# Attention steps in pairs with two products per step, in place of 64 by 64 quarters

## The chip, the cores and the metric

The kernel runs on one core of one Trainium2 chip. The metric is the device time of one execution in microseconds (us), the median of three runs before the change: 3099.51 us (3098.32 to 3102.71). A core has five engines that run their own instruction queues: PE (matrix products; its weight loads are listed as PEld), DVE (vector), ACT (scalar functions), POOL (general) and SP (which here only issues DMA transfers). Each instruction queue is executed in its order; instructions wait for each other through semaphores.

## The reference

The input is a batch of 8 images of 512 channels by 32 x 32 pixels. Two residual layers follow each other; each computes its output from a group-normalised copy of its input and adds it to that input.

- Layer 0: a group norm, a 1x1 convolution with SiLU (`cv1`), then two bottleneck blocks l = 0, 1. A block is a 3x3 convolution with SiLU, an attention over the 1024 pixels with 4 heads of 64 channels, a 1x1 convolution with SiLU and a residual add. All parts are concatenated and go through a last 1x1 convolution (`cv2`).
- Layer 1: a group norm, a depthwise 3x3 convolution with ReLU, a pruning of weak channels, a 1x1 convolution with ReLU and a second pruning.

The attention is what the change touches:

```
logits = jnp.einsum('bhdi,bhdj->bhij', q, k + r) * HD ** (-0.5)
a = jax.nn.softmax(logits, axis=-1)
out = jnp.einsum('bhij,bhdj->bhdi', a, v)
```

## The kernel before

Everything is fp32. One image is processed at a time. Inside a tile the 128 partitions are channels or, for the attention's exponentials, key pixels. Each fp32 product appears in the trace as two passes (two weight loads and two matmul records).

**The loop over images.** For image b: `cv1`; then for l = 0 and l = 1 the 3x3 convolution `conv3`, the projections `qkv`, `attention` and `cv2m`; between the second `qkv` and the second attention the back of layer 1 for the image before (`layer1_back`), and loads of the next image; then `cv2`. After the loop the last image's layer 1 runs alone.

**Background work.** The front of layer 1 of the previous image (49 pieces: four statistics, one group reduction, four applies, and for each of four channel blocks one start, eight taps and one end) and the group norm of the next image (nine pieces) are lists of closures. `pump` takes pieces off a list between PE instructions: six times per half of `conv3` (one piece each), after each of the six tiles of `qkv` (two pieces), and after each of the four tiles of `cv2` (three pieces). The end of a channel block is a ReLU on ACT, a maximum on DVE and a product on POOL. The group reduction needs two tiny PE products (`pm`, `pv`) with DVE work between them and after them.

**Scheduling.** The tile framework orders each engine's instructions by program order and its own priorities and gives tiles to buffers when it builds the program. So the order on each engine and every wait is fixed before the run; a piece from `pump` may stand somewhat earlier or later than it was written, and it holds its place in its engine's queue.

**Attention.** One call has 32 steps (m, ih, jt): m is a pair of heads, ih one half of the query pixels, jt one of eight blocks of 128 key pixels. Eight steps with one (m, ih) are called a group here; four groups make a call, and 16 calls make the kernel. A step has

- a score product into a PSUM tile of two banks (`ps_s`, from the pool `ps_big` with two buffers), L440: four 64 by 64 quarters of the PE array, one per head a and half c of the key block;
- one exponential of 128 x 1024 on ACT into a tile e of the shared `work` pool (8 buffers), L448;
- one addition of e to the running sum on DVE, L455 (L452 for the first two of a group);
- a value product, L466, for the step two before: again four quarters. The two halves r of the contraction go to two accumulators (`ps_acc`, three buffers).

At a group's end ACT copies one accumulator to SBUF (L476), DVE adds the other to it (L478), and two steps later `finish` multiplies the sums by a matrix of ones (`ps_dn`, L485: two products of 128 rows by 64 columns side by side), copies the denominators by ACT (L490, which also accumulates them for a range check), takes the reciprocal on DVE (L491), passes it once more through ACT for the range check (L492), and scales on DVE (L496).

**Around attention.** `cv2m` (L516) follows at once; its SiLU on ACT needs another function table than the exponential. DVE then adds the residual (L525), which releases the PSUM tile. After l = 0 the transform of `conv3` follows on DVE (L326 to L339); after l = 1 `cv2` (L538) takes the released tile.

Of the kernel before, what the change touches and what calls it, by code (L numbers as in the profile page):

```python
# [8 lines left out]
F32 = mybir.dt.float32  # L9
AF = mybir.ActivationFunctionType  # L10
ALU = mybir.AluOpType
AX = mybir.AxisListType

P = 128
B, C, F = 8, 512, 32
HW = F * F
# [14 lines left out]
def fast_kernel(  # L31
# [21 lines left out]
    dram = ctx.enter_context(tc.tile_pool(name="dram", bufs=1, space=bass.MemoryType.DRAM))  # L53
    small = ctx.enter_context(tc.tile_pool(name="small", bufs=4))
    ps_big = ctx.enter_context(tc.tile_pool(name="ps_big", bufs=2, space=bass.MemoryType.PSUM))
    ps_acc = ctx.enter_context(tc.tile_pool(name="ps_acc", bufs=3, space=bass.MemoryType.PSUM))
    ps_mm = ctx.enter_context(tc.tile_pool(name="ps_mm", bufs=1, space=bass.MemoryType.PSUM))

    def const_tile(shape, name):
        return const.tile(shape, F32, tag=name, name=name)  # L60

    def work_tile(name):
        return workp.tile([P, HW], F32, tag="work", name=name)
# [45 lines left out]
    ones = const_tile([P, HD], "ones")  # L109
    nc.gpsimd.memset(ones, 1.0)  # L110

    rng = const_tile([P, 2 * B * 2 * HEADS], "rng")
    rng_used = [0]
    mhalf = const_tile([P, NBN], "mhalf")
    nc.gpsimd.memset(mhalf, -0.5)
# [267 lines left out]
    def qkv(l, bg, per):  # L383
        for m in range(4):
            ps = ps_big.tile([P, 2, 512], F32, tag="big", name="ps_qk")
            for k in range(2):
                for n in range(2):
                    nc.tensor.matmul(  # L388
                        ps[:, n, :],
                        wqkv_sb[:, k, m * P : (m + 1) * P],  # L390
                        z[:, k, n * 512 : (n + 1) * 512],
                        start=(k == 0),
                        stop=(k == 1),
                    )
            if m < 2:
                nc.scalar.copy(qy[:, m, :], flat(ps))
            else:
                kk = phases(kr[:, m - 2, :])
                full = [P, 4, F, F // 4]
                col = rw[:, l, m - 2, :].rearrange("p (t r) -> p r t", r=4)  # L400
                row = rh[:, l, m - 2, :].unsqueeze(1).unsqueeze(3)
                nc.vector.tensor_tensor(
                    kk, phases(flat(ps)), col.unsqueeze(2).to_broadcast(full), ALU.add
                )
                nc.gpsimd.tensor_tensor(kk, kk, row.to_broadcast(full), ALU.add)
            pump(bg, per)
        for g in range(2):
            ps = ps_big.tile([P, 4, C2], F32, tag="big", name="ps_v")
            for j in range(4):
                jt = 4 * g + j  # L410
                for k in range(2):
                    nc.tensor.matmul(  # L412
                        ps[:, j, :],
                        z[:, k, jt * P : (jt + 1) * P],
                        wqkv_sb[:, k, 2 * C2 : 3 * C2],
                        start=(k == 0),
                        stop=(k == 1),
                    )
            nc.scalar.copy(vt[:, 4 * g : 4 * g + 4, :], ps)
            pump(bg, per)  # L420

    def attention():

        last = HW // P - 1
        steps = [(m, ih, jt) for m in range(2) for ih in range(2) for jt in range(HW // P)]
        es, sm, accs = {}, {}, {}
        quarters = [(r, c) for c in range(2) for r in range(2)]  # L430

        def half(r):
            return slice(r * HD, (r + 1) * HD)

        def scores(s):
            m, ih, jt = steps[s]
            ps = ps_big.tile([P, 2, 512], F32, tag="big", name="ps_s")
            for a, c in quarters:
                j = jt * P + c * HD
                nc.tensor.matmul(  # L440
                    ps[half(c), a, :],
                    kr[half(a), m, j : j + HD],
                    qy[half(a), m, ih * 512 : (ih + 1) * 512],
                    start=True,
                    stop=True,
                )
            e = work_tile("e").rearrange("p (a n) -> p a n", a=2)
            nc.scalar.activation(flat(e), flat(ps), AF.Exp, scale=HD ** -0.5)  # L448
            es[s] = e
            if jt == 1:  # L450
                sm[m, ih] = work_tile("sum").rearrange("p (a n) -> p a n", a=2)
                nc.vector.tensor_tensor(flat(sm[m, ih]), flat(es[s - 1]), flat(e), ALU.add)  # L452
            elif jt:
                t = flat(sm[m, ih])
                nc.vector.tensor_tensor(t, t, flat(e), ALU.add)  # L455

        def values(s):
            m, ih, jt = steps[s]
            if jt == 0:
                accs[m, ih] = [  # L460
                    ps_acc.tile([P, 512], F32, tag="acc", name=f"ps_av{r}") for r in range(2)
                ]
            e = es.pop(s)
            for r, a in quarters:
                h = 2 * m + a
                nc.tensor.matmul(  # L466
                    accs[m, ih][r][half(a), :],
                    vt[half(r), jt, h * HD : (h + 1) * HD],
                    e[half(r), a, :],
                    start=(jt == 0),  # L470
                    stop=(jt == last),
                )
            if jt == last:
                lo, hi = accs.pop((m, ih))
                part = work_tile("part")[:, :512]
                nc.scalar.copy(part, hi)  # L476
                zz = z[:, m, ih * 512 : (ih + 1) * 512]
                nc.vector.tensor_tensor(zz, lo, part, ALU.add)  # L478

        def finish(s):  # L480
            m, ih, _ = steps[s]
            dn = ps_mm.tile([P, 512], F32, tag="mm", name="ps_dn")
            t = sm.pop((m, ih))
            for a in range(2):
                nc.tensor.matmul(dn[half(a), :], ones, t[:, a, :], start=True, stop=True)  # L485

            n = rng_used[0]
            rng_used[0] += 2
            r = work_tile("r")
            nc.scalar.activation(r[:, 512:], dn, AF.Copy, accum_out=rng[:, n : n + 1])  # L490
            nc.vector.reciprocal(r[:, :512], r[:, 512:])  # L491
            nc.scalar.activation(  # L492
                r[:, 512:], r[:, :512], AF.Copy, accum_out=rng[:, n + 1 : n + 2]
            )
            zz = z[:, m, ih * 512 : (ih + 1) * 512]
            nc.vector.tensor_tensor(zz, zz, r[:, :512], ALU.mult)  # L496

        for s in range(len(steps) + 4):
            if s < len(steps):
                scores(s)  # L500
            if 2 <= s < len(steps) + 2:
                values(s - 2)
            if s >= 4 and steps[s - 4][2] == last:
                finish(s - 4)

    def pump(bg, n):

        for _ in range(min(n, len(bg))):
            bg.pop(0)()
# [14 lines left out]
            dst = inner(yp[1], m) if l == 0 else phases(qy[:, m, :])  # L524
            nc.vector.tensor_tensor(dst, phases(flat(ps)), inner(yp[l], m), ALU.add)  # L525

    def cv2(bg, per):
        def rhs(k, n):
            i, m = k // 2, k % 2
            if i in (1, 2):  # L530
                return yp[i - 1][:, 2 * n : 2 * n + 2, m, :, : F // 4]
            return (y0 if i == 0 else qy)[:, m, n * 512 : (n + 1) * 512]

        for m in range(KC):
            ps = ps_big.tile([P, 2, 512], F32, tag="big", name="ps_cv2")
            for k in range(2 * KC):
                for n in range(2):
                    nc.tensor.matmul(  # L538
                        ps[:, n, :],
                        w2_sb[:, k, m * P : (m + 1) * P],  # L540
                        rhs(k, n),
                        start=(k == 0),
                        stop=(k == 2 * KC - 1),
                    )
            act(flat(ps), flat(ps), AF.Silu, BN1 + m)
            nc.vector.tensor_tensor(by_phase(xt[m]), phases(flat(ps)), by_phase(xt[m]), ALU.add)  # L546
            pump(bg, per)

    for w in group_norm(pt, pt):
        w()  # L550
# [1 line left out]
    for b in range(B):  # L552
        cv1()

        bg = layer1_front() if b else []
        conv3(0, bg, 1)
        load_weights(1)
        qkv(0, bg, 2)
        load_qkv(1)
        attention()  # L560
        cv2m(0)
        conv3(1, bg, 1)
        if b + 1 < B:
            load_weights(0)
        qkv(1, bg, 2)
        load_qkv(0)
        pump(bg, len(bg))
        if b:
            layer1_back(b - 1)
        load(xt, b)  # L570
        if b + 1 < B:
            load(pt, b + 1)
            bg = group_norm(pt, pt)
        attention()
        cv2m(1)
        cv2(bg, 3)
        pump(bg, len(bg))
    for w in layer1_front():
        w()
    layer1_back(B - 1)  # L580
# [463 lines left out]
```

## Time and profile before

| What | us |
|---|---|
| median of three runs | 3099.51 |
| time of the profiled execution | 3102.71 |
| span of the profiled execution, first to last instruction | 3100.9 |
| PE busy | 2863.0 (92%) |
| DVE busy | 1858.2 (60%) |
| ACT busy | 988.7 (32%) |
| score products, 4096 records | 557.1 busy, 72.0 idle before them |
| value products, 4096 records | 546.3 busy |

Busy time is the union of an engine's instructions. A row of a timeline merges neighbouring records of one line: its second column is the time from the start of the first to the end of the last of them, and since matmuls overlap, the distance between starts tells how long one takes. The idle time in brackets is followed by what released the engine.

### The profile page before, as it was taken

How to read it: one execution, taken by the hardware profiler on the slowest of the kernel's cores; microseconds unless marked ns; L12 is line 12 of the kernel's file. 1: busy time of each engine (PE TensorE's matmuls, PEld its weight loads, DVE VectorE, ACT ScalarE, POOL GpSimd, SP SyncE). 2: the span in 40 equal slices, each digit the busy share in tenths (PEclk: the TensorE clock that was granted, in tenths of full speed). 3: DMA queues.
4: the chain of work that ended last, by engine and by line, in shares of the span. 5: the costliest groups of instructions: out<-in, count | busy, mean ns of one | idle time of the engine just before them, and what ended most of it. 6: DMA issues, size and time to landing. Idle time of an engine off the chain costs nothing. (4 is left out here: it accounts for less than half of the span.)

```text
span 3100.9 us, 32925 instructions
## 1 busy us (share of the span) xinstructions
PE 2863.0 (92%) x14146; PEld 1448.0 (47%) x14146; DVE 1858.2 (60%) x1995; ACT 988.7 (32%) x1153; POOL 137.0 (4%) x89
## 2 busy tenths in 40 slices
PE   6999999999999999999999999999999999999984
PEld 4453463534645345543555436463363633636331
DVE  6546268572685627756278553775447664576637
ACT  1425124251242413334143331524215241152511
POOL 1000010000100001000010000100001000000000
PEclk9999999999999999999999999999999999999996
DMA  8110010300104001030011200112010120100100
GB/s 348 62 62 11 1 71 1 139 15 0 71 4 149 1 0 72 31 122 1 1 72 62 92 1 31 42 62 92 0 52 21 72 82 1 61 11 24 42 0 28
DMA packets 27513, 155.81 MB, mean 50 GB/s; under 512 B 2784, under 2 KB 7648, under 8 KB 23008
## 3 DMA queue, kind: packets, MB, share of 16 engines
q1 hardware_dynamic: 26352, 149.17, 13.1%
q10 hardware_dynamic: 1008, 4.46, 0.4%
q8 instruction: 113, 1.85, 0.2%
q14 instruction: 40, 0.33, 0.0%
HBM read 127.41 MB, written 26.21 MB: 50 GB/s over the span
## 5 line engine op out<-in xcount | busy, mean ns | idle before, releaser
L440 PE MATMUL ps_s<-qy,kr 64*64 64x512 f32 x4096 | 557.1, 608 | 72.0 <-ACT e L448 36.7
L448 ACT ACTIVATE e<-ps_s 128x1024 f32<-128x1024 f32 x512 | 516.8, 1021 | 246.1 <-PE ps_s L440 246.0
L466 PE MATMUL ps_av<-e,vt 64*64 64x512 f32 x4096 | 546.3, 595 | 0.0
L455 DVE TENSOR_TENSOR sum<-sum,e 128x1024 f32<-128x1024 f32 x384 | 467.0, 1216 | 87.5 <-ACT e L448 75.8
L353 PE MATMUL ps_c<-v,u_sb 128*128 128x248 f32 (+1 forms) x1536 | 350.2, 390 | 42.8 <-issue 39.2
L353 PEld LDWEIGHTS ps_c<-v,u_sb 128*128 128x128 f32 x1536 | 305.2, 199 | 91.1 <-issue 53.3
L440 PEld LDWEIGHTS ps_s<-qy,kr 64*64 64x64 f32 x4096 | 159.7, 135 | 384.2 <-issue 235.2
L250 DVE SCALAR_TENSOR_TENSOR acc<-pt,v_sb,acc 128x961 f32<-128x961 f32 (+1 forms) x256 | 318.9, 1257 | 5.9
L466 PEld LDWEIGHTS ps_av<-e,vt 64*64 64x64 f32 x4096 | 177.8, 134 | 275.0 <-issue 255.7
L546 DVE TENSOR_TENSOR xt<-ps_cv,xt 128x1024 f32<-128x1024 f32 x32 | 64.2, 2005 | 355.5 <-ACT ps_cv L141 355.5
L273 PE MATMUL ps_pw<-pt,wpw_sb 128*128 128x512 f32 x512 | 226.0, 602 | 41.3 <-POOL pt L261 40.6
L491 DVE RECIPROCAL r<-r 128x512 f32<-128x512 f32 x64 | 214.6, 3353 | 26.6 <-ACT r L490 26.6
L388 PE MATMUL ps_qk<-z,wqkv_sb 128*128 128x512 f32 x512 | 224.2, 594 | 5.7 <-ACT z L375 5.7
L292 PE MATMUL ps_cv<-pt,w_sb 128*128 128x512 f32 x512 | 224.1, 599 | 2.3 <-DVE pt L229 2.3
L538 PE MATMUL ps_cv<-yp,w_sb 128*128 128x512 f32 x512 | 224.9, 592 | 0.0
L141 ACT ACTIVATE ps_cv<-ps_cv,bi,sc 128x1024 f32<-128x1024 f32 x32 | 37.7, 1177 | 450.3 <-PE ps_cv L538 450.3
L452 DVE TENSOR_TENSOR sum<-e 128x1024 f32<-128x1024 f32 x64 | 78.4, 1225 | 168.0 <-ACT e L448 168.0
L273 PEld LDWEIGHTS ps_pw<-pt,wpw_sb 128*128 128x128 f32 x512 | 98.8, 194 | 163.7 <-issue 120.3
L353 PE MATMUL ps_c3e<-v,u_sb 128*128 128x248 f32 (+1 forms) x768 | 170.7, 376 | 0.0
L292 PEld LDWEIGHTS ps_cv<-pt,w_sb 128*128 128x128 f32 x512 | 98.3, 192 | 126.3 <-issue 123.4
L538 PEld LDWEIGHTS ps_cv<-yp,w_sb 128*128 128x128 f32 x512 | 97.3, 190 | 122.5 <-issue 122.5
L388 PEld LDWEIGHTS ps_qk<-z,wqkv_sb 128*128 128x128 f32 x512 | 96.7, 190 | 123.6 <-issue 108.7
(137 smaller groups left out, 2345.3 us busy)
## 6 DMA issues: line engine op xcount, KB each, us to landing
u_sb<-u SPq DMA_DIRECT2D x30, 2304.0 KB, 8.1
pt<-in_x SPq DMA_DIRECT2D x32, 512.0 KB, 5.7
xt<-in_x SPq DMA_DIRECT2D x32, 512.0 KB, 3.6
out<-xt SPq DMA_DIRECT2D x32, 512.0 KB, 2.9
wqkv_sb<-in_wqkv SPq DMA_DIRECT2D x16, 768.0 KB, 4.3
u<-u_sb SPq DMA_DIRECT2D x1, 4608.0 KB, 14.2
u<-ustage SPq DMA_DIRECT2D x18, 256.0 KB, 5.2
w_sb<-in_w SPq DMA_DIRECT2D x1, 2048.0 KB, 16.5
```

Source lines behind the costliest of these rows:

```text
L250: nc.vector.scalar_tensor_tensor(o, i, dw[:, c, t : t + 1], o, ALU.mult, ALU.add)
L273: nc.tensor.matmul(ps[:, n, :], wpw_sb[:, k, m * P : (m + 1) * P], pt[k][:, n * 512 : (n + 1) * 512], start=(k == 0), stop=(k == KC - 1),)
L292: nc.tensor.matmul(ps[:, n, :], w1_sb[:, k, m * P : (m + 1) * P], pt[k][:, n * 512 : (n + 1) * 512], start=(k == 0), stop=(k == KC - 1),)
L353: nc.tensor.matmul(o[:, to : to + n], u_sb[:, m, p, dy, k * P : (k + 1) * P], v[:, k * 256 + of : k * 256 + of + n], start=(i == 0), stop= ...
L388: nc.tensor.matmul(ps[:, n, :], wqkv_sb[:, k, m * P : (m + 1) * P], z[:, k, n * 512 : (n + 1) * 512], start=(k == 0), stop=(k == 1),)
L440: nc.tensor.matmul(ps[half(c), a, :], kr[half(a), m, j : j + HD], qy[half(a), m, ih * 512 : (ih + 1) * 512], start=True, stop=True,)
L448: nc.scalar.activation(flat(e), flat(ps), AF.Exp, scale=HD ** -0.5)
L452: nc.vector.tensor_tensor(flat(sm[m, ih]), flat(es[s - 1]), flat(e), ALU.add)
L455: nc.vector.tensor_tensor(t, t, flat(e), ALU.add)
L466: nc.tensor.matmul(accs[m, ih][r][half(a), :], vt[half(r), jt, h * HD : (h + 1) * HD], e[half(r), a, :], start=(jt == 0), stop=(jt == last),)
L491: nc.vector.reciprocal(r[:, :512], r[:, 512:])
L538: nc.tensor.matmul(ps[:, n, :], w2_sb[:, k, m * P : (m + 1) * P], rhs(k, n), start=(k == 0), stop=(k == 2 * KC - 1),)
```

## The change

- A score product is now two instructions per step instead of four: one for each head, with 64 rows and 128 columns of the array. A value product is two instructions instead of four: one for each head, with 128 rows and 64 columns. One accumulator per group takes the place of two; the copy and the addition at a group's end (L476, L478) are gone.
- Steps are taken two at a time: two score products, then the two value products of the pair before.
- `finish` has no work on ACT: DVE takes the reciprocal from PSUM, a DVE operation with an accumulator takes the place of the two range accumulations, and DVE multiplies the accumulator by the reciprocal.
- `ps_acc` has two buffers instead of three, `ps_mm` two instead of one.
- `attention` now takes background pieces: one at every fourth step in the first call, and one at every third step in the second. `qkv` takes one piece per tile instead of two; `cv2` takes none.

```diff
-    ps_acc = ctx.enter_context(tc.tile_pool(name="ps_acc", bufs=3, space=bass.MemoryType.PSUM))
-    ps_mm = ctx.enter_context(tc.tile_pool(name="ps_mm", bufs=1, space=bass.MemoryType.PSUM))
+    ps_acc = ctx.enter_context(tc.tile_pool(name="ps_acc", bufs=2, space=bass.MemoryType.PSUM))
+    ps_mm = ctx.enter_context(tc.tile_pool(name="ps_mm", bufs=2, space=bass.MemoryType.PSUM))
...
-    def attention():
+    def attention(bg, every):
...
-            for a, c in quarters:
-                j = jt * P + c * HD
+            for a in range(2):
+                r = slice(a * HD, (a + 1) * HD)
                 nc.tensor.matmul(
-                    ps[half(c), a, :],
-                    kr[half(a), m, j : j + HD],
-                    qy[half(a), m, ih * 512 : (ih + 1) * 512],
+                    ps[:, a, :],
+                    kr[r, m, jt * P : (jt + 1) * P],
+                    qy[r, m, ih * 512 : (ih + 1) * 512],
...
-                accs[m, ih] = [
-                    ps_acc.tile([P, 512], F32, tag="acc", name=f"ps_av{r}") for r in range(2)
-                ]
+                accs[m, ih] = ps_acc.tile([P, 512], F32, tag="acc", name="ps_av")
             e = es.pop(s)
-            for r, a in quarters:
+            for a in range(2):
                 h = 2 * m + a
                 nc.tensor.matmul(
-                    accs[m, ih][r][half(a), :],
-                    vt[half(r), jt, h * HD : (h + 1) * HD],
-                    e[half(r), a, :],
+                    accs[m, ih][a * HD : (a + 1) * HD, :],
+                    vt[:, jt, h * HD : (h + 1) * HD],
+                    e[:, a, :],
...
-            if jt == last:
-                lo, hi = accs.pop((m, ih))
-                part = work_tile("part")[:, :512]
-                nc.scalar.copy(part, hi)
-                zz = z[:, m, ih * 512 : (ih + 1) * 512]
-                nc.vector.tensor_tensor(zz, lo, part, ALU.add)
...
-            r = work_tile("r")
-            nc.scalar.activation(r[:, 512:], dn, AF.Copy, accum_out=rng[:, n : n + 1])
-            nc.vector.reciprocal(r[:, :512], r[:, 512:])
-            nc.scalar.activation(
-                r[:, 512:], r[:, :512], AF.Copy, accum_out=rng[:, n + 1 : n + 2]
-            )
-            zz = z[:, m, ih * 512 : (ih + 1) * 512]
-            nc.vector.tensor_tensor(zz, zz, r[:, :512], ALU.mult)
-
-        for s in range(len(steps) + 4):
-            if s < len(steps):
-                scores(s)
-            if 2 <= s < len(steps) + 2:
-                values(s - 2)
-            if s >= 4 and steps[s - 4][2] == last:
-                finish(s - 4)
+            r = work_tile("r")[:, :512]
+            nc.vector.reciprocal(r, dn)
+            n = rng_used[0]
+            rng_used[0] += 1
+            nc.vector.scalar_tensor_tensor(
+                t[:, 0, :], dn, 1.0, r, ALU.mult, ALU.add, accum_out=rng[:, n : n + 1]
+            )
+            nc.vector.tensor_tensor(
+                z[:, m, ih * 512 : (ih + 1) * 512], accs.pop((m, ih)), r, ALU.mult
+            )
+
+
+        last = HW // P - 1
+        for s in range(0, len(steps) + 4, 2):
+            for t in (s, s + 1):
+                if t < len(steps):
+                    scores(t)
+            for t in (s - 2, s - 1):
+                if 0 <= t < len(steps):
+                    values(t)
+            if s >= 4 and steps[s - 3][2] == last:
+                finish(s - 3)
+            for t in (s, s + 1):
+                if t % every == 0:
+                    pump(bg, 1)
...
-    def cv2(bg, per):
+    def cv2():
...
-            pump(bg, per)
...
-        qkv(0, bg, 2)
+        qkv(0, bg, 1)
         load_qkv(1)
-        attention()
+        attention(bg, 4)
...
-        qkv(1, bg, 2)
+        qkv(1, bg, 1)
...
-        attention()
+        attention(bg, 3)
+        pump(bg, len(bg))
         cv2m(1)
-        cv2(bg, 3)
-        pump(bg, len(bg))
+        cv2()
```

## The prediction

> **What bounds the kernel now.** I read the page's busy table and costliest groups first, then a timeline of one attention call, then the joints after it.
>
> ```profile
> PE 2863.0 (92%) x14146; PEld 1448.0 (47%) x14146; DVE 1858.2 (60%) x1995; ACT 988.7 (32%) x1153; POOL 137.0 (4%) x89
> L440 PE MATMUL ps_s<-qy,kr 64*64 64x512 f32 x4096 | 557.1, 608 | 72.0 <-ACT e L448 36.7
> L466 PE MATMUL ps_av<-e,vt 64*64 64x512 f32 x4096 | 546.3, 595 | 0.0
> L491 DVE RECIPROCAL r<-r 128x512 f32<-128x512 f32 x64 | 214.6, 3353 | 26.6 <-ACT r L490 26.6
> ```
>
> PE is the bound, and attention is over a third of it. The timeline of a call (image 2, l = 0), at a group's end, a little later, and at the call's end:
>
> ```profile
> 849.92 1.04 PE L440 MATMUL ps_s<-qy,kr 64*64 64x512 f32 x8
> 850.78 1.04 PE L466 MATMUL ps_av<-e,vt 64*64 64x512 f32 x8
> ...
> 855.31 1.08 PE L485 MATMUL ps_dn<-sum,ones 128*64 128x512 f32 x4
> 856.32 1.09 PE L440 MATMUL ps_s<-qy,kr 64*64 64x512 f32 x8
> 857.23 1.04 PE L466 MATMUL ps_av<-e,vt 64*64 64x512 f32 x8
> ...
> 862.23 1.09 PE L440 MATMUL ps_s<-qy,kr 64*64 64x512 f32 x8 [0.53 <-ACT e L448]
> ...
> 898.84 0.30 PEld L516 LDWEIGHTS ps_m<-z,wm_sb 128*128 128x128 f32 x2 [0.81 <-issue]
> 899.37 0.19 PEld L516 LDWEIGHTS ps_m<-z,wm_sb 128*128 128x128 f32 x1 [0.24 <-issue]
> 899.80 0.19 PEld L516 LDWEIGHTS ps_m<-z,wm_sb 128*128 128x128 f32 x1 [0.24 <-issue]
> ```
>
> Starts are 0.86 us apart: a product costs 0.86 whether score or value, two passes of 0.43 with four quarters side by side, and all weight loads hidden. Only at a group's end is something lost: the ones product changes the array's shape twice, and exponentials stand behind the copies on ACT (0.53 shown). Now the joints:
>
> ```profile
> 997.75 3.33 PE L440 MATMUL ps_s<-qy,kr 64*64 64x512 f32 x16 [4.91 <-DVE xt L284]
> 1065.99 1.28 ACT L141 ACT_TABLE_LOAD   x1
> 1069.08 0.39 PE L224 MATMUL pv<-d,g_sb 128*128 128x4 f32 x2 [0.85 <-DVE d L222]
> 1070.86 0.81 DVE L229 TENSOR_SCALAR pt<-pt,gm,rs 128x1024 f32<-128x1024 f32 x1 [1.20 <-POOL rs L226]
> 1072.86 5.09 PE L538 MATMUL ps_cv<-y,w_sb 128*128 128x512 f32 x8 [3.40 <-DVE qy L525]
> 2955.87 3.70 PE L538 MATMUL ps_cv<-y,w_sb 128*128 128x512 f32 x8 [1.67 <-DVE qy L525]
> ```
>
> Before `cv2` the next image's group norm holds up the residual add on DVE; the last image, without it, waits 1.67 only. After idle stretches of 3.4 or more, products first run at half pace: 8 records took 5.09 against 3.70, 16 took 3.33 against 1.88.
>
> **What the skill says.** The Trainium skill, "TensorEngine Tiling (Array Packing)", Key Properties: a change of tiling mode drains the array. The trace agrees: the ones product took 1.01 from start to start instead of 0.86. "TensorE: Matmul & The Clock Gate", Part 1: about 3.4 us of idleness halve PE's clock; the 3.33 row agrees. The same page, "Architectural detail": ACT and DVE are strict FIFO; the trace agrees: the exponential behind ACT's group-end copies was late, and PE with it (0.53). "ScalarE: Activation LUTs", "What ACT_TABLE_LOAD costs": about 1283 ns a load; the row says 1.28.
>
> **The change part by part.** Waits and order come from the changed program's fixed instruction order, durations from rows of before.
>
> *Products: nothing gained.* Each is still two passes over half arrays side by side. The ones product is the trace's case of two 128 by 64 halves: 4 records at the pace of 0.86. I take 0.86 for the row halves of 64 by 128 too; the trace lacks that shape. Bounds: 0.76 if fewer instructions save something, 1.72 if the halves don't overlap.
>
> *Shape changes: new.* In 1.01 − 0.86 = 0.15 a drain of about 0.1 and 0.05 of exposed load lie; the first pass after a change to 128-column weights took 0.53, not 0.43, so 0.1 is exposed there. A change into values costs 0.14, into scores 0.19. A call has 15 of the first and 14 of the second (ones products follow values in the same shape): 2.1 + 2.7 = 4.8.
>
> *One call.* Bare work: 68 products × 0.858 = 58.3, and 1.8 of initial waiting for the first exponential: 60.1. Before, the call ran from 834.35 to 898.84 = 64.5, so 4.4 was lost at its four group ends. Afterwards 4.8, plus 0.1 at the start (the fourth score waits for the second exponential), 0.2 for leaving, and 1.0 before the last ones product: DVE needs, from the start of the ones product before, 1.1 + 3.35 (reciprocal) + 4 sums × 1.3 + 2 × 0.7 = 11.1, while PE arrives after 10.1. So 6.1: 1.7 more, × 16 calls = **+27**. The ACT work that goes (five instructions a group) gives its gain in the 4.4; the rest of it was behind PE.
>
> *Taps in the first call of images 1 to 7.* The scheduler puts channel block 1 (start, eight taps) among DVE's first eleven sums, and its ReLU on ACT between exponentials 10 and 11, waiting for the last tap. Behind it stand exponential 11, then score 13, which needs its PSUM buffer, then all of PE. These rows give the paces:
>
> ```profile
> 944.36 8.88 DVE L250 SCALAR_TENSOR_TENSOR acc<-pt,v_sb,acc 128x992 f32<-128x992 f32 x7
> 1024.35 3.88 DVE L455 TENSOR_TENSOR sum<-sum,e 128x1024 f32<-128x1024 f32 x3
> ```
>
> Taps 1.27, sums 1.3 each. From the call's start, PE takes a pair every 2 × 1.72 + 0.33 = 3.76: pairs begin at 7.3, 11.1, 14.9, 18.6, and after a ones product at 23.25; score 13 is due at 24.1. On DVE, sum 4 waits for its exponential to 9.6; from there eight tiles of work follow almost without rest: sum 4 and start to 11.6, sum 5 and two taps to 15.4, sum 6 and tap to 18.0, sum 7 to 19.3, three taps to 23.1, the next group's sum to 24.4, two taps to 27.0. ReLU (1.24) to 28.3, exponential (1.02) to 29.3, score 13 at 29.4: **5.3 late**. A gap of that size makes PE cold; rows above lost 1.4 and more (16 records, 3.33 against 1.88), I take 2.4 since the cold stretch can cover more records. 7 × 7.7 = **+54**. Nothing later in the call is late: the following buffers and the accumulator of group 2 are free before PE comes to them. If ReLU were not behind the taps, this term would be zero.
>
> *Group norm in the second call of images 0 to 6.* Statistics stay where they were, ahead of the sums. `pm` now stands after a value pair, and `pv` between the two halves of a score product. From the start of the first ones product T, DVE works 1.3 (sum), 3.35, 1.3, 0.7, 0.7, 1.3, then gm and three tiny steps 0.8, and `pv` can go at T + 9.3; PE gets there at T + 6.9. So 2.4 of waiting, 0.9 for the score's halves no longer running together, 0.9 for extra shape changes and the tiny products: 4.2 × 7 = **+29**. Gone is its part ahead of `cv2`: from the start of the last `ps_m` record to `cv2` 5.34 (1067.52 to 1072.86), in the last image 2.26 (2953.61 to 2955.87); and the cold start of 1.4: −4.5 × 7 = −31.
>
> *Function table.* Before, range copies on ACT made the SiLU table load early: 1065.99 to 1067.27, ready with `ps_m`. Now the load itself carries the wait for the first finished `ps_m` tile, and adds 1.1 to all 16 joints: +18. Its cover was the wait for PE.
>
> *Smaller.* The `kr` additions no longer stand behind taps (0.8 before L412, seven times, −6); one more tap stands ahead of y at L371 (+0.6 × 7 = +4). Buffers of `ps_acc` and `ps_mm`: two suffice in the order above. No DMA moves; the next image's load keeps its place on SP.
>
> Sum: 27 + 54 + 29 − 31 + 18 − 2 = **+95**, that is 3100.9 + 95 = 3196 of span. The profiled execution took 3102.7, 1.8 around its span and 3.2 over the median, so the median should be 3099.5 + 95 = 3195.
>
> **Rivals.**
> 1. *DVE saturates.* In the first calls DVE has 28 sums, 18.8 for four group ends and 11 of taps, that is 65 of some 74; `work` has eight buffers for four e, two sums, r and acc. If exponentials wait for buffers through all calls, say 5 each: 80 more, 3275. Against it: most of the calls have no taps. 0.12.
> 2. *The ReLU does not block*, because taps find room in DVE's early waits: −54, 3141. Against it: the fixed order. 0.10.
> 3. *Row halves run one after the other*: 0.86 × 512 = 440 more, 3635. Against it: quarters in different rows do overlap now. 0.04.
> 4. *Not slower:* the wider products save more than everything above. With half as many instructions each of 1024 products must shrink by 95 / 1024 = 0.093, to below 0.765, to reach the old time; at 0.71 the result is 3044. Against it: the ones product has this form and took the full two passes. 0.05.
> That the change doesn't do what it says is excluded by the program's order: pairs stand there.
>
> **How the numbers follow.** 0.69 goes to the sum, whose own range is 3160 to 3230 (±14 from 2 us in the tap stall, ±20 from 0.05 in 464 shape changes). With rivals 1 and 2, 0.91 lies between 3135 and 3275; shaving their outer edges, the range is 3137 to 3265. A difference of 0.2% (6 us) is what can be told from none. Rival 4's 0.05 is 0.04 of faster and 0.01 of same; rival 2 with cheaper shape changes adds 0.01 to same. Slower: 0.94.
>
> **What would show it.** Right: PE starts in pairs with 0.86 inside and about 1.0 across shape changes; a gap near 5 us at one L433 product of seven first calls, released by ACT; a gap near 2.4 at L224 in seven second calls; ACT's table load starting after `ps_m`. Wrong: score pairs much off 0.86, no such gaps, or idle PE at most exponentials.

## The result and the profile after

The kernel after takes 3204.23 us (median of four runs, 3199.2 to 3208.12) against 3101.11 us for the kernel before in the same comparison (3098.32 to 3106.33): a ratio of 1.033, 95% interval 1.0309 to 1.0351. It is slower by 103 us; 3195 was forecast. The profiled execution of after has a span of 3197.3 us, 96.4 more than the 3100.9 of before, and the trace readings below are made against that difference.

The page of after, engines and three of the costliest groups (busy, mean ns of one | idle before, releaser):

```profile
PE 2949.9 (92%) x10050; PEld 1428.5 (45%) x10050; DVE 1852.0 (58%) x2059; ACT 852.5 (27%) x833; POOL 137.0 (4%) x89
...
L433 PE MATMUL ps_s<-qy,kr 64*128 64x512 f32 x2048 | 545.5, 641 | 71.8 <-ACT e L441 35.8
...
L457 PE MATMUL ps_av<-e,vt 128*64 128x512 f32 x2048 | 512.7, 625 | 0.0
```

Half as many instructions, and PE is busy 87 us longer: the busy column can't show a gain or loss of pace here, since records overlap and a record at half pace counts double. Stages do. In this table, worked out from the trace, a stage reaches from its first PE record to the first of the next stage (the last `cv2` up to the last image's own layer 1); sums over eight images, us:

| Stage | before | after | difference |
|---|---|---|---|
| first attention calls | 515.9 | 573.1 | +57.2 |
| second attention calls | 555.2 | 601.0 | +45.8 |
| `cv2m` and the wait behind it, l = 0 | 96.3 | 107.0 | +10.7 |
| the same, l = 1 | 91.9 | 81.1 | −10.8 |
| `conv3`, both | 510.4 | 515.3 | +4.9 |
| `qkv`, first | 180.9 | 175.3 | −5.6 |
| `cv2` | 489.9 | 484.7 | −5.2 |

All other rows are within 0.5. So the difference lies in the attention calls and at their ends. The first call of image 0, without background pieces, takes 65.96 in place of 64.50; those of images 1 to 7 take 72.41 to 72.51 in place of 64.49. The timeline of image 2, where the call began at 845.42 (columns: start, us from the first start to the last end, engine, line, operation; in brackets the idle time before and its releaser):

```profile
862.71 1.22 DVE L448 TENSOR_TENSOR sum<-sum,e 128x1024 f32<-128x1024 f32 x1
863.84 3.79 DVE L250 SCALAR_TENSOR_TENSOR acc<-pt,v_sb,acc 128x992 f32<-128x992 f32 x3
...
868.68 2.50 DVE L250 SCALAR_TENSOR_TENSOR acc<-pt,v_sb,acc 128x992 f32<-128x992 f32 x2
868.85 1.13 PE L433 MATMUL ps_s<-qy,kr 64*128 64x512 f32 x4
871.10 1.22 DVE L448 TENSOR_TENSOR sum<-sum,e 128x1024 f32<-128x1024 f32 x1
871.22 1.24 ACT L141 ACTIVATE pt<-acc,bi,sc 128x1024 f32<-128x1024 f32 x1 [4.81 <-DVE acc L250]
872.37 1.92 ACT L441 ACTIVATE e<-ps_s 128x1024 f32<-128x1024 f32 x2
...
873.42 2.08 PE L433 MATMUL ps_s<-qy,kr 64*128 64x512 f32 x4 [3.44 <-ACT e L441]
...
875.43 3.68 PE L457 MATMUL ps_av<-e,vt 128*64 128x512 f32 x8
```

ACT stood idle 4.81 us at the ReLU until DVE had done the last tap; one exponential later PE's second score of the pair could go, 3.44 us late. And then 8 value records took 3.68 where they otherwise take 1.94: half pace.

The second call of the same image, around the group reduction:

```profile
1047.24 0.39 PE L217 MATMUL pm<-mv,g_sb 128*128 128x4 f32 x2
1047.56 1.98 PE L433 MATMUL ps_s<-qy,kr 64*128 64x512 f32 x6
1051.06 0.38 PE L224 MATMUL pv<-d,g_sb 128*128 128x4 f32 x2 [1.53 <-DVE d L222]
1051.38 1.12 PE L433 MATMUL ps_s<-qy,kr 64*128 64x512 f32 x2
1052.43 2.89 PE L457 MATMUL ps_av<-e,vt 128*64 128x512 f32 x8
1055.25 2.68 PE L433 MATMUL ps_s<-qy,kr 64*128 64x512 f32 x8
```

`pv` waits 1.53 us in the middle of a score product, and the next two pairs of products are slow as well (2.89 against 1.94, 2.68 against 1.99).

The ends of the two calls of image 2:

```profile
917.93 7.13 PE L509 MATMUL ps_m<-z,wm_sb 128*128 128x512 f32 x16
...
924.28 1.28 ACT L141 ACT_TABLE_LOAD   x1 [10.01 <-PE ps_m L509]
925.58 2.27 ACT L141 ACTIVATE ps_m<-ps_m,bi,sc 128x1024 f32<-128x1024 f32 x2
...
931.30 2.04 PE L353 MATMUL ps_c<-v,u_sb 128*128 128x256 f32 x4 [6.24 <-issue]
```

```profile
1101.13 5.35 PE L531 MATMUL ps_cv<-y,w_sb 128*128 128x512 f32 x8 [3.01 <-DVE qy L518]
```

The table load starts only when the first `ps_m` tile is done, and everything behind it moves by 1.34 us (13.37 for the stage, 12.03 before). Ahead of `cv2` the gap is 3.01 in place of 3.40, and its first 8 records still take 5.35.

### The profile page after: what moved, and what is told of

Same layout as the page of the kernel before. It is cut to its first block, busy times and chain, and to the rows that moved or that the text cites. A ratio compares the mean times of both kernels' runs of the same rounds, so it can differ in the third digit from the quotient of the medians.

```text
span 3197.3 us, 24563 instructions
## 1 busy us (share of the span) xinstructions
PE 2949.9 (92%) x10050; PEld 1428.5 (45%) x10050; DVE 1852.0 (58%) x2059; ACT 852.5 (27%) x833; POOL 137.0 (4%) x89
## 4 chain that ended last, share of the span: by engine, by line
PE 77%; DVE 13%; ACT 4%; issue 3%; DMA 2%; POOL 0%; SPq 0%; ACTq 0%; DVEq 0%; POOLq 0%
PE ps_cv L531 14%; PE ps_s L433 13%; PE ps_av L457 11%; PE ps_c L353 9%; PE ps_qk L388 6%; PE ps_cv L292 6%; PE ps_pw L273 6%; DVE acc L250 5%; PE ps_c3e L353 4%; PE ps_v L412 3%; DVE sum L448 3%; PE ps_m L509 3%; ACT e L441 2%; PE ps_dn L470 1%; DMA pt<-in_x 1%
## 5 line engine op out<-in xcount | busy, mean ns | idle before, releaser
L441 ACT ACTIVATE e<-ps_s 128x1024 f32<-128x1024 f32 x512 | 499.4, 1022 | 534.1 <-PE ps_s L433 533.6
L433 PE MATMUL ps_s<-qy,kr 64*128 64x512 f32 x2048 | 545.5, 641 | 71.8 <-ACT e L441 35.8
L457 PE MATMUL ps_av<-e,vt 128*64 128x512 f32 x2048 | 512.7, 625 | 0.0
L433 PEld LDWEIGHTS ps_s<-qy,kr 64*128 64x128 f32 x2048 | 183.1, 193 | 414.1 <-issue 226.9
L457 PEld LDWEIGHTS ps_av<-e,vt 128*64 128x64 f32 x2048 | 129.0, 140 | 354.4 <-issue 349.8
L474 DVE RECIPROCAL r<-ps_dn 128x512 f32<-128x512 f32 x64 | 214.8, 3356 | 18.9 <-PE ps_dn L470 18.9
L388 PEld LDWEIGHTS ps_qk<-z,wqkv_sb 128*128 128x128 f32 x512 | 96.7, 190 | 125.4 <-issue 107.0
L353 PEld LDWEIGHTS ps_c3e<-v,u_sb 128*128 128x128 f32 x768 | 144.9, 190 | 15.9
```

The lines of the kernel that those rows point to most:

```text
L353: nc.tensor.matmul(o[:, to : to + n], u_sb[:, m, p, dy, k * P : (k + 1) * P], v[:, k * 256 + of : k * 256 + of + n], start=(i == 0), stop= ...
L388: nc.tensor.matmul(ps[:, n, :], wqkv_sb[:, k, m * P : (m + 1) * P], z[:, k, n * 512 : (n + 1) * 512], start=(k == 0), stop=(k == 1),)
L433: nc.tensor.matmul(ps[:, a, :], kr[r, m, jt * P : (jt + 1) * P], qy[r, m, ih * 512 : (ih + 1) * 512], start=True, stop=True,)
L457: nc.tensor.matmul(accs[m, ih][a * HD : (a + 1) * HD, :], vt[:, jt, h * HD : (h + 1) * HD], e[:, a, :], start=(jt == 0), stop=(jt == HW // ...
L474: nc.vector.reciprocal(r, dn)
```

## The experiments

Ratios are to the kernel before, timed in the same comparison, with 95% intervals. Stage times are of the profiled execution of each kernel, which can lie some us off the median. Line numbers differ between kernels.

### The taps in the first call

Without them:

```diff
-        qkv(0, bg, 1)
+        qkv(0, bg, 2)
-        attention(bg, 4)
+        attention([], 4)
-        qkv(1, bg, 1)
+        qkv(1, bg, 2)
```

> The kernel after, but no background piece in the first attention call, and two per tile in qkv as in the kernel before. Theory (the ReLU at the end of channel block 1 stands among the exponentials and waits for taps): the first calls of images 1 to 7 fall from 72.4 us to that of image 0, 66.0, so 7 x 6.4 = 45 us less; the kr additions stand behind taps again, +6. In all about 3204 - 40 = 3164 us (3155 to 3172). Rival (DVE is too full in the whole call, taps or not, or the pairs themselves cost the time): the calls stay above 70 us and the total above 3190. On PE no gap over 2 us is left inside a first call under the theory.

Measured: 3159.33 us, ratio 1.0185 (1.017 to 1.0201), 45 us less than after. First calls: 66.33 for image 1 and 65.96 for images 2 to 7, `qkv` +5.6 as expected. The place of these pieces is the cause. They can reach PE in two ways: through ACT's queue, in which the ReLU waits for the last tap, or through DVE's backlog, which gives buffers back late. The next run tells them apart:

```diff
-                act(pt[c], box.pop("acc"), AF.Relu, BN4 + c)
+                if c == 1:
+                    n = BN4 + c
+                    nc.vector.tensor_scalar(
+                        pt[c], box.pop("acc"), sc[:, n : n + 1], bi[:, n : n + 1], ALU.mult, ALU.add
+                    )
+                    nc.vector.tensor_scalar(pt[c], pt[c], 0.0, None, ALU.max)
+                else:
+                    act(pt[c], box.pop("acc"), AF.Relu, BN4 + c)
```

> The kernel after with one edit: the ReLU that ends channel block 1 is two DVE operations (scale and add, then maximum with 0) in place of one on ACT. All taps keep their place on DVE. Theory (ACT's queue is what carries the lateness of the taps to PE): the 3.44 us gap at a score product of the first calls of images 1 to 7 goes and with it the cold stretch; these calls fall from 72.4 to 66 to 68 us, in all 28 to 45 us less than 3204, about 3166. Rival (the backlog on DVE itself holds PE, because sums free the exponentials' buffers too late): the gap stays at 2 us or more, or moves to a later score product, and the total stays within 12 us of 3204; DVE even has 1.7 us more to do in each of these calls.

Measured: 3165.6 us, ratio 1.0204 (1.0187 to 1.0222), 39 us less than after; first calls of images 1 to 7 take 67.62 to 67.97. The same place in its timeline:

```profile
872.11 0.81 DVE L259 TENSOR_SCALAR pt<-acc,sc,bi 128x1024 f32<-128x1024 f32 x1
872.50 1.13 PE L440 MATMUL ps_s<-qy,kr 64*128 64x512 f32 x4
872.83 1.22 DVE L455 TENSOR_TENSOR sum<-sum,e 128x1024 f32<-128x1024 f32 x1
873.01 1.94 ACT L448 ACTIVATE e<-ps_s 128x1024 f32<-128x1024 f32 x2 [2.10 <-DVE pt L259]
...
874.09 1.13 PE L440 MATMUL ps_s<-qy,kr 64*128 64x512 f32 x4 [0.46 <-ACT e L448]
875.15 1.94 PE L464 MATMUL ps_av<-e,vt 128*64 128x512 f32 x8
```

DVE does the same taps at the same time and two operations more. PE waits 0.46, not 3.44, and the records behind run at full pace. So ACT's queue carried most of the lateness: what costs is a ReLU that waits among the exponentials. Part of the rest over 65.96 (1.66 us) is the other way, by DVE: an exponential waits 2.10 (873.01) for the DVE operation that frees the buffer of `acc`, and PE 0.46 behind it.

### The group reduction in the second call

`pm` with its DVE work stays one piece, `pv` with the rest becomes the next, three steps later:

```diff
-        work.append(groups)
+        if dst is src:
+            work += [groups, groups2]
+        else:
+            work.append(lambda: (groups(), groups2()))
```

(`groups2` holds `pv` and what follows it; `dst is src` is the next image's group norm.)

> The kernel after with the group reduction of the next image's group norm as two pieces: pm with its DVE work, and three steps later pv. Theory (PE reaches pv before DVE has d): the 1.53 us gap at pv goes in seven second calls, 11 us, the two halves of the score product run together again, 3 us, and half-pace products behind the gap go where they appeared: 3204 - 17 = 3187 us (3178 to 3193); the second calls of images 0 to 6, now 72.4 to 76.6 us, come down to 70 to 72. Rival (the tiny products themselves and DVE's extra pieces cost the time): within 6 us of 3204, the second calls unchanged, because pm and pv now change the array's form in two places.

Measured: 3169.32 us, ratio 1.0215 (1.0201 to 1.0229), 35 us less than after, twice what was expected. The timeline, image 2:

```profile
1043.58 0.38 PE L219 MATMUL pm<-mv,g_sb 128*128 128x4 f32 x2
1043.90 1.99 PE L442 MATMUL ps_s<-qy,kr 64*128 64x512 f32 x8
1045.81 1.94 PE L466 MATMUL ps_av<-e,vt 128*64 128x512 f32 x8
1047.68 0.39 PE L230 MATMUL pv<-d,g_sb 128*128 128x4 f32 x2
1048.00 1.99 PE L442 MATMUL ps_s<-qy,kr 64*128 64x512 f32 x8
```

No gap, no half pace, and from the start of a tiny product to the next product only 0.32 each. The seven second calls get 2.2 to 6.4 us shorter each, 28.7 in all. How a call starts differs from run to run; counted from its first ones product, image 0, where no slow records followed `pv` in the kernel after, gains 2.64: the wait of 1.53 and 1.1 for the broken score product. Four images gain 4.3 and two 5.9 there: what they gain more, 13 us in all, is half-pace products behind `pv`. The profiled execution as a whole is 22.7 shorter only, since its `cv2` took 6.4 more, at half pace behind the same 3.01 gap in all eight images.

### The function table

```diff
+            if s == len(steps) - 2:
+                warm = small.tile([P, 1], F32, tag="warm", name="warm")
+                nc.scalar.activation(warm, es[s + 1][:, 0, :1], AF.Silu)
```

> The kernel after with one activation more per attention call: a SiLU of one column of the last exponential, right behind it on ACT, so that the function table is loaded while PE still works on the last values. Theory (the load carries the wait for the first finished ps_m tile and stands ahead of its SiLU): the way from cv2m to the next PE product gets 1.3 us shorter in 16 joints, 21 us, and up to 8 us of half-pace products go with the shorter gap: 3204 - 25 = 3179 us (3173 to 3185). Rival (the joint waits for PE or DVE and the load is beside it): within 6 us of 3204, and the gap ahead of conv3 stays at 6.2 us.

Measured: 3156.44 us, ratio 1.017 (1.0156 to 1.0183), 48 us less than after. ACT, image 2:

```profile
909.26 1.28 ACT L492 ACT_TABLE_LOAD   x1
910.56 0.20 ACT L492 ACTIVATE warm<-e 128x1 f32<-128x1 f32 x1
919.21 2.27 ACT L141 ACTIVATE ps_m<-ps_m,bi,sc 128x1024 f32<-128x1024 f32 x2 [8.45 <-PE ps_m L512]
```

The load is over 8.45 us before it is needed. All 16 joints (from `cv2m` to the next stage) are 1.34 shorter (21.4). In the profiled run, 39.7 shorter, most of the rest is half pace that went: `cv2` 8.4 (its gap is 1.67, and images 0 to 6 take 55.04), `conv3` 7.3. First calls take 7.2 less and second calls 3.7 more, where products behind `pv` now run slow in all seven images. I had allowed 8 for half pace in all.

### The two halves of the change, each alone

The products, pairs and finish with all pieces in their old places, and the reverse: the quarters and single steps of before with the pieces in their new places.

```diff
 kernel after:                          kernel before:
-        attention(bg, 4)               -        attention()
+        attention([], 4)               +        attention(bg, 4)
-        attention(bg, 3)               -        attention()
-        pump(bg, len(bg))              +        attention(bg, 3)
-        cv2()                          +        pump(bg, len(bg))
+        attention([], 3)               -        cv2(bg, 3)
+        cv2(bg, 3)                     +        cv2()
...                                     ...
```

(Left out: both `qkv` calls take two pieces per tile on the left and one on the right, and `attention` and `cv2` take or lose their arguments for pieces.)

> The kernel after with all background pieces where the kernel before has them: two per tile of qkv, none in the attention calls, three per tile of cv2. So the new products, pairs and finish alone. Theory (calls cost 66.0 us in place of 64.5 where nothing else is in them, and the function table is late): 16 x 1.46 = 23 for the calls, 16 x 1.34 = 21 for the table, some 8 us of half-pace products behind the longer gaps ahead of conv3: 3102 + 52 = 3154 us (3145 to 3162). First calls 66.0, second calls of images 0 to 6 near 69. Rival (the placement of pieces is what costs, the products nothing): within 10 us of 3102. Other rival (products cost more than read from image 0): above 3170.

> The kernel before with only the placement of background pieces changed as in the kernel after: one per tile of qkv, one at every fourth step of the first attention call, one at every third of the second, none in cv2. Theory (costs of pieces and products add): it makes up the rest of the 103 us, 103 - 52 = about +50, 3150 us, with first calls of images 1 to 7 near 71 us and a gap at a score product behind the ReLU, and second calls up by about 5. Rival (the lateness needs the faster start of the new calls; here PE loses 4.4 us at group ends anyway and the taps fit in): first calls stay below 67 and the total is near the old time or below it, 3085 to 3110, because the group norm ahead of cv2 is gone.

Measured: products alone 3145.38, ratio 1.0137 (1.0122 to 1.0152), +42 where +52 was expected; pieces alone 3169.07, ratio 1.021 (1.0191 to 1.0228), +66 where some +50 was. Products alone: first calls 65.95 to 65.96 as expected, but the late table costs nothing after l = 1 in seven images (11.94 against 11.88): there the next image's group norm on DVE ends later still. It and the table wait are not a sum but a maximum.

Pieces alone cost more than I worked out from the difference, and by another way:

```profile
866.68 1.24 ACT L141 ACTIVATE pt<-acc,bi,sc 128x1024 f32<-128x1024 f32 x1 [7.58 <-DVE acc L250]
867.82 1.00 ACT L448 ACTIVATE e<-ps_s 128x1024 f32<-128x1024 f32 x1
...
868.73 0.57 ACT L476 COPY part<-ps_av 128x512 f32<-128x512 f32 x1
...
869.35 1.12 PE L466 MATMUL ps_av<-e,vt 64*64 64x512 f32 x3 [7.08 <-ACT part L476]
```

The ReLU now stands two exponentials earlier (behind nine of the call in place of eleven), and behind it also the copy that empties an accumulator, for which a value product waits: 7.08 us in place of 3.44. That 42 + 66 comes near 103 is thus no proof that the halves add: the pieces cost a first call some 10 us here and 6.5 in the kernel after. How much of that the copy makes is not shown, since the ReLU's place differs too.

### Twice as many changes of shape

```diff
-        for s in range(0, len(steps) + 4, 2):
-            for t in (s, s + 1): ... scores(t)
-            for t in (s - 2, s - 1): ... values(t)
...
+        for s in range(len(steps) + 4):
+            if s < len(steps): scores(s)
+            if 2 <= s < len(steps) + 2: values(s - 2)
...
```

> The kernel after with its steps one at a time (score s, value s - 2, score s + 1, ...) in place of pairs, so that the array changes its shape about 59 times a call and not 29. Theory (0.14 us for a change into values, 0.19 into scores): 15 x 0.14 + 15 x 0.19 = 5.0 us more in the first call of image 0, 66.0 to about 70.5 once the wait for the last sum is off; PE comes later to score 13, so the gap there falls to about 1.7 us. In all 16 x 4.5 = 72 more, less some 15: 3204 + 57 = 3260 us (3235 to 3285). Rival (the drain is paid once per exponential, not per change, or pairs save nothing): the first call of image 0 stays within 1 us of 66.0 and the total below 3220.

Measured: 3216.1 us, ratio 1.0376 (1.036 to 1.0392). The price is right: image 0's first call takes 70.79, 4.83 more for 30 more changes, 0.161 each where (0.14 + 0.19) / 2 = 0.165 stood; the wait of 0.25 before the last ones product is gone in exchange, so the bare price is a little higher. Its timeline:

```profile
115.26 1.08 PE L457 MATMUL ps_av<-e,vt 128*64 128x512 f32 x4
116.27 1.13 PE L433 MATMUL ps_s<-qy,kr 64*128 64x512 f32 x4
117.33 1.08 PE L457 MATMUL ps_av<-e,vt 128*64 128x512 f32 x4
```

One product and one change take 1.01 and 1.06, against 0.86 bare: 0.15 and 0.20. The total was missed by 44 us and lies where the rival had put it, below 3220; but the rival's first call within 1 us of 66.0 is not there. In first calls the gap behind the ReLU shrinks to 1.03, and its half-pace stretch goes entirely: those calls take 71.97 to 72.25, no more than in pairs. The larger part of this is a change of order that I had not foreseen: the ReLU stands behind ten exponentials of the call in place of eleven, and its last tap is done 24.0 us after the call's start in place of 25.8. PE itself comes only 0.6 later to the score behind it. In second calls the wait at `pv` falls from 1.53 to 0.16, with no half pace behind it, and image 0's call grows by 3.48, not by 4.83: a loss on the way to a wait is paid once, not twice.

### The change mended, and the kernel before with what was good in it

Early table, split group reduction, no pieces in the first call, all in the kernel after:

> The kernel after with the three mends together: no piece in the first attention call and two per tile of qkv, pm and pv as two pieces three steps apart in the second call, and the early load of the SiLU table. What stays of the change is the half-array products in pairs with the DVE finish. Theory (the three costs are separate, beside 1.46 us a call for products, changes of shape and finish): first calls 66.0, second calls of images 0 to 6 near 72, cv2m joints 12.0 and 8.8, cv2 at 55.0: about 3097 us (3085 to 3108), the old time within 0.4%. Against the quarters with the same move of the group norm (3086 us) it stays some 11 us longer. Rival (the costs replace each other: with one wait gone another comes up): above 3120.

Measured: 3096.33 us, ratio 0.9981 (0.9974 to 0.9988). First calls 65.96 but for image 1 (66.33), second calls of images 1 to 6 71.86 to 73.41, image 0's 66.59. The three costs are as good as gone, and the kernel is back at the old time, below it by about 0.2%, the least that can be told.

The quarters with only the group norm moved (edit: `attention(bg, 3)` with the split reduction for the second call, `cv2` without pieces):

> The kernel before with one move: the next image's group norm is taken in the second attention call (every third step), with pm and pv as two pieces three steps apart, and not in cv2. Theory: the joint ahead of cv2 falls from 3.40 to 1.67 us of gap and cv2 starts at full pace (4.5 us in 7 images, 31 us less), against about 1.5 us in each second call for two tiny products and their changes of shape (11 us more): 3102 - 20 = 3082 us (3072 to 3092). Rival (pieces of the group norm on DVE hold up the sums and with them PE): second calls grow by over 4 us and the total is at 3100 or above.

Measured: 3086.09, ratio 0.9949 (0.9937 to 0.996). `cv2` takes 55.04 in images 0 to 6, second calls grow by 15 in all. Then the finish of after in these quarters:

```diff
-            nc.scalar.activation(r[:, 512:], dn, AF.Copy, accum_out=...)
-            nc.vector.reciprocal(r[:, :512], r[:, 512:])
-            nc.scalar.activation(r[:, 512:], r[:, :512], AF.Copy, accum_out=...)
+            nc.vector.reciprocal(r[:, :512], dn)
+            nc.vector.scalar_tensor_tensor(t[:, 0, :], dn, 1.0, r[:, :512], ..., accum_out=...)
...
+            if s == len(steps) - 1:
+                warm = small.tile([P, 1], F32, tag="warm", name="warm")
+                nc.scalar.activation(warm, es[s][:, 0, :1], AF.Silu)
```

> The kernel before with the move of the group norm as in the run ahead of it, and finish as in the kernel after: the reciprocal from PSUM and the range sum on DVE, no copies of denominators by ACT; a SiLU of one column right behind the last exponential loads the function table early. The 64 by 64 quarters and single steps stay. Theory (half of the 4.4 us lost at the four group ends of a call is exponentials behind ACT's copies): calls get 2.2 us shorter, 16 x 2.2 = 35, so 3082 - 35 = 3047 us (3035 to 3065). Rival (DVE becomes the bound at group ends: it gets 0.7 us more per group, 3.35 + 3 x 0.7 + 7 x 1.3 = 14.6 for 14.6 of PE work): calls keep 64 us or grow, and the total stays at 3075 to 3090.

Measured: 3078.69, ratio 0.9924 (0.9912 to 0.9936): faster than both kernels, but short of the 3035 to 3065 that was expected and within what the rival gave. First calls take 62.98 to 62.99, 1.5 less than before, where 2.2 was expected. The exponentials no longer wait behind ACT's second range copy, which waited for the reciprocal (first row, of the kernel before):

```profile
860.54 0.63 ACT L492 ACTIVATE r<-r 128x512 f32<-128x512 f32 x1 [2.04 <-DVE r L491]
...
847.90 1.08 PE L494 MATMUL ps_dn<-sum,ones 128*64 128x512 f32 x4
...
849.37 3.35 DVE L499 RECIPROCAL r<-ps_dn 128x512 f32<-128x512 f32 x1
...
850.07 1.02 ACT L457 ACTIVATE e<-ps_s 128x1024 f32<-128x1024 f32 x1 [1.87 <-PE ps_s L449]
```

In exchange the last ones product of a call waits 1.13 for DVE's sum, in place of 0.25: that much of the rival holds. Second calls were 6.7 us longer in all than with the copies, which I laid to DVE's extra work. The last run tests that; it keeps ACT's copies in second calls only.

> The quarters in single steps with the group norm in the second call and the early table, as in the run without ACT copies, but the DVE finish in first calls only; second calls keep the copies by ACT. Theory (the DVE finish gains 1.5 us where DVE has nothing else, and loses 0.8 us on average where it also has the group norm): first calls 63.0, second calls 72, 3078.7 - 7 = 3072 us (3065 to 3079). Rival (the second calls of the two runs differ by half-pace products that fall as they fall): within 3 us of 3078.7.

Measured: 3080.45, ratio 0.9933 (0.992 to 0.9947): nothing gained. Its second calls sum to 581.3, even more than 577.3. So the finish on DVE is not, as a whole, what makes them longer. The timelines show that each finish has one wait of its own there, first the run without copies, then the last one:

```profile
1391.16 0.35 PE L219 MATMUL pm<-mv,g_sb 128*128 128x4 f32 x2 [1.99 <-DVE sum L500]
...
1782.47 1.09 PE L450 MATMUL ps_s<-qy,kr 64*64 64x512 f32 x8 [2.05 <-ACT e L458]
```

Without copies `pm` waits for DVE's range sum, which reads the denominators: these kernels have one `ps_mm` buffer, which both need (the kernel after has two). With copies the pieces of the group norm hold up the reciprocal, and an exponential stands behind ACT's copy again. The two waits are nearly equal, so the finish makes little difference to these calls. The rival, half-pace products falling as they fall, fits what is left: behind the wait they appear in five of seven images without copies and in six with them.

## Why the prediction was right, step by step

The sum of +95 met a measured +96.8 over the stages. The mechanisms were the ones named; several terms were mis-sized, and their errors cancelled in part: that the total came so near is partly luck.

| Term as predicted | predicted | measured |
|---|---|---|
| one call, 16 × 1.7 | +27 | +23 (16 × 1.46) |
| taps, 7 × 7.7 | +54 | +45 (7 × 6.5) |
| group norm in the second call, 7 × 4.2 | +29 | +35 (7 × 3.3, half pace behind `pv` 13, call starts −1) |
| group norm gone ahead of `cv2`, 7 × 4.5 | −31 | −28 (gap 21.6, pace 6.7) |
| function table, 16 × 1.1 | +18 | +21 (16 × 1.34) |
| smaller | −2 | −8 (`kr` −5.6; first `conv3` of image 0 −1.2; second call of image 7 −1.2) |
| half pace in `conv3` of l = 1 and in the last `cv2` | none | +8 |

- **Products.** 0.86 for row halves was right. These rows of after, image 2, show it: the weights of both heads are loaded together, and the passes follow 0.43 apart (853.39 to 853.82), 0.86 for a product. So rival 3 (3635) and rival 4 (3044) fall, and the ones product was a fair model.

```profile
852.85 1.99 PE L433 MATMUL ps_s<-qy,kr 64*128 64x512 f32 x8
853.39 0.19 PEld L433 LDWEIGHTS ps_s<-qy,kr 64*128 64x128 f32 x2 [0.24 <-issue]
853.82 0.19 PEld L433 LDWEIGHTS ps_s<-qy,kr 64*128 64x128 f32 x2 [0.23 <-issue]
...
854.77 1.94 PE L457 MATMUL ps_av<-e,vt 128*64 128x512 f32 x8
...
856.64 1.99 PE L433 MATMUL ps_s<-qy,kr 64*128 64x512 f32 x8
```

- **Shape changes.** 0.14 and 0.19 nearly hold: a pair of scores and a pair of values take 3.79 from start to start (852.85 to 856.64), where 3.76 stood.
- **One call.** 1.46, found unaltered in three kernels with the first calls clear of pieces (image 0 of after, the run without taps, products alone). Within it two terms were off and nearly cancel: the last ones product comes 0.4 late and not 1.0, and the changes of shape come to about 5.2 and not 4.8 (what is left of the 5.9 over bare work).
- **Taps.** The way (last tap, ReLU, exponential 11, score 13) is shown by the two runs; rival 2 falls. DVE's backlog by itself, rival 1's way, is 1.7 of the 6.5 at most. The size was off: the stall is 3.44, not 5.3. Score 13 started 28.0 us after the call's start in place of 29.4, and was due at 24.56 in place of 24.1. The early start is mostly DVE: I let sums cost 1.3 each, and in a full queue they follow at 1.13 (862.71 to 863.84). The half pace behind it was 3.0, not 2.4.
- **Group norm in the second call.** The three terms named came to 3.3, not 4.2: the wait at `pv` was 1.53, not 2.4, again mostly through the pace of sums (1.07 and 1.13; besides, the terms listed for `pv` add to 9.45, not to 9.3). What I left out cost more, 13 us: half pace behind so short a wait, in six of the seven images. The step that failed is the addition of three terms (wait, broken product, changes) with none for pace.
- **Ahead of `cv2`.** I took the cold start of 1.4 as gone with the group norm. With the table's 1.34 on top the gap is 3.01, and `cv2` started at half pace in five of eight images, the last among them, which had run at full pace before (+1.5). The two terms were worked out apart and act on the same gap.
- **Function table.** Right in kind, 1.34 for 1.1; through half pace, in `conv3` and `cv2` above all, it costs nearly as much again, as its run shows (39.7 in the profiled run, 48 by the medians).
- **Smaller.** `kr` −5.6 for −6. The +4 at L371 isn't there: first `conv3` takes 30.89 in images 1 to 7 of both.
- **Rival 1** (DVE saturates) falls: image 0's call, in which DVE has all sums and finishes, loses 1.46 and no more, and calls with taps wait in one place only.

## What to carry to other kernels

When background work is placed, look for the one instruction of it that goes through another engine's in-order queue: here 11 us of taps on DVE cost a call at most 1.7 us, and one ReLU behind them on ACT cost 4.8 more in each of seven calls. When the last user of a function table goes off the end of a stage, put a tiny activation there, or the load lands behind the wait for the next input. And add the terms that act on one gap before you price its effect on PE's pace: a loss on the way to a wait comes off that wait, and a gap made shorter is worth more than its length where products behind it ran at half pace.

## What was not expected of the hardware

- PE falls to half pace behind much shorter gaps than I had assumed. After the 1.53 us wait at `pv`, slow records followed in six of seven images, at once or some products later, and with that wait gone in none; gaps of 3.01 ahead of `cv2` had them in five of eight (in four to eight of eight in other runs), gaps of 1.67 there in none of the kernels that have it. The Trainium skill, "TensorE: Matmul & The Clock Gate", Part 1, says that activity is watched in a free-running window of about 3.4 us, which fits that equal gaps end differently; its section "Why this matters for your kernels" advises to keep gaps below about 3 us, and here 1.53 was enough. The measurement decides.
- DVE's reciprocal of 128 x 512 takes as long from PSUM as from SBUF (3356 ns on average after, 3353 before), so the copies ahead of it bought no time there.
- Second calls of one kernel differ by some us from image to image (72.87 to 75.18 for images 1 to 6 in the run without ACT copies), where first calls repeat to 0.02. Part is half pace. Another part is a load: the call's second score waits for the last residual add of `layer1_back`, and ahead of that add DVE has statistics of the next image, which wait for the DMA transfer of `pt`. The call of image 1 began at 606.70, that of image 3 at 1357.48:

```profile
609.82 1.29 DVE L212 BATCH_NORM_STATS2 st<-pt 128x6 f32<-128x512 f32 x2 [0.46 <-DMA pt<-in_x]
613.88 2.84 PE L449 MATMUL ps_s<-qy,kr 64*64 64x512 f32 x12 [6.10 <-DVE xt L293]
...
1359.25 1.29 DVE L212 BATCH_NORM_STATS2 st<-pt 128x6 f32<-128x512 f32 x2 [0.76 <-DMA pt<-in_x]
1363.31 3.69 PE L449 MATMUL ps_s<-qy,kr 64*64 64x512 f32 x16 [4.75 <-DVE xt L293]
```

The statistics start 3.12 and 1.77 us into the call, and PE goes on 4.06 after them both times, as in the other images. When the load lands is thus carried to PE through DVE's queue, as the taps were through ACT's; no run here moves those statistics.
